# Ten unread products on TensorE between the first expert layer and the second attention

## The chip, the cores and the metric

The kernel runs on one core of one Trainium2 chip. The metric is the device time of one launch in microseconds (us). A core has five engines that work at the same time, each through its own queue in order: TensorE (PE, matrix products; its weight loads stand apart as PEld), VectorE (DVE), ScalarE (ACT), GpSimd (POOL) and SyncE (SP, which here only starts DMAs). [...]

## The reference

A network of two layers over 2708 tokens of width 256. Each layer is an attention over a graph given by the integer matrix adj (2708 x 2708, about 1.2% ones), and then a mixture of eight experts of which each token uses two. Both add to x, and both take x after a layer norm.

```python
# layer 0
x = x + elu(softmax(where(adj > 0, q k.T / 16, -9e15)) @ v)      # q, k, v of layernorm(x)
x = x + sum over a token's two best experts of w * (gelu(LN(x) W1 + b1) W2 + b2)   # hidden 1024
# layer 1
H = layernorm(x) @ W_fc + b_fc
s = (H @ w_att[:256])[:, None] + (H @ w_att[256:])[None, :] + b_att
x = x + softmax(where(adj > 0, s, -1e9), axis=1) @ H
x = x + sum over the two best experts, as above                    # hidden 512
```

In the second attention the first term of s is the same for a whole row, so it drops out of the softmax: the weight of a key is exp of its own score, masked by adj. The products of the change stand in none of these lines. What they compute is read by nobody.

## The kernel before, in words

**Tiling.** Tokens are cut into 22 tiles of up to 128 rows (NT), the last with 20. The first attention runs over blocks of 512 queries; the second over five groups of 6, 6, 4, 3 and 3 query tiles (GROUPS), each group going through all 22 key tiles, with one PSUM accumulator for each query tile. The expert layers run over slots: a slot is up to 128 tokens of one expert, whose rows are fetched from a table in DRAM (disp).

**Between the layers.** Each slot of the first expert layer ends with a scatter that adds its rows to xd0 in DRAM (L1197, on POOL's queue). `experts0.run` does 45 slots and, by a branch on a count, up to five more. `layer1_attention` then opens its pools over the memory of the layer that has ended: `kept` and `att1` on the right side of SBUF. `normed_rows` (L613) loads a tile of xd0 into kept (L615, SP), takes its statistics (L205 to L207, DVE), has POOL raise two numbers to the power -1/2 (L211), and writes the normalised tile xn (L217, DVE; four buffers, L617).

**The first group** does more than attend. For each key tile k, `columns` (L621) turns xn on TensorE (L223, two transposes against the identity `ident`), ACT copies the result out of PSUM into xT (L224), and DVE adds up its rows (L628). `values` (L631) multiplies xT by wfc (L635). ACT takes the exponent of one column (L641) and scales the rows by it (L642), and writes the part of the router (L643). POOL adds a bias to kept (L647) and makes the upper part of the rows (L650), DVE the rest (L652). `attend` (L677), three key tiles behind (LAG1), multiplies the masks by both parts (L685), which ACT has cast from one byte to float32r (L673). The loop is written so that the norm is two tiles ahead and the transpose one.

```python
            ahead = [normed_rows(t) for t in range(2)]
            cols = columns(0, ahead.pop(0))
```

The change stands just ahead of these two lines (L716, L717).

**What sets the order.** SP's instructions keep the order of the code (`manual_schedule` at L79). Inside `layer1_attention` the orders of TensorE, DVE, ACT and POOL are made by the framework's planner when the kernel is built: [...] nothing of the attention moves ahead of the end of the first expert layer. [...]

**PSUM.** The pool misc has two buffers of one bank (128 x 512 float32). Transposes, L635 and small products take turns in it. The accumulators of the second attention have six banks of their own.

**After the first group** the raw sums are divided and routed (`evict`, `finish`, `Experts.route`), tile by tile beside the next group's products, and scattered into the second layer's table (L950, POOL).

Of the kernel before, what the change touches and what calls it, by code (L numbers as in the profile page):

```python
# [9 lines left out]
F32 = mybir.dt.float32  # L10
# [10 lines left out]
P = 128  # L21
# [13 lines left out]
GROUP = 4  # L35
# [11 lines left out]
GROUPS = [6, 6, 4, 3, 3]  # L47

FIRST_MASKS = 2


FULL_AFTER = {14: 20, 16: 24}
# [13 lines left out]
def adj_ffn_kernel(ctx: ExitStack, tc: tile.TileContext, a: dict, out: bass.AP):  # L66
    nc = tc.nc
# [9 lines left out]
    misc = ctx.enter_context(tc.tile_pool(name="misc", bufs=2, space=PSUM))  # L77
# [4 lines left out]
    ident = const.tile([P, P], F32, name="ident")  # L82
# [117 lines left out]
    def norm_stats(src, r, deviation=None):  # L200

        st = small.tile([P, 6], F32, name="ln_st")
        mv = small.tile([P, 2], F32, name="ln_mv")
        rs = small.tile([P, 2, 2], F32, name="ln_rs")
        nc.vector.bn_stats(st[:r], src)  # L205
        nc.vector.bn_aggr(mv[:r], st[:r])
        nc.vector.scalar_tensor_tensor(  # L207
            rs[:r, 0], once_twice[:r, 0], mv[:r, 1:2], once_twice[:r, 1],
            op0=ALU.mult, op1=ALU.add,
        )  # L210
        nc.gpsimd.tensor_tensor(rs[:r, 1], rs[:r, 0], minus_half[:r], ALU.pow)  # L211
        if deviation is not None:
            nc.vector.tensor_mul(deviation, rs[:r, 0, 0:1], rs[:r, 1, 0:1])
        return mv[:r, 0:1], rs[:r, 1, 0:1], rs[:r, 1, 1:2]

    def normed(dst, src, mean, factor):
        nc.vector.tensor_scalar(dst, src, mean, factor, op0=ALU.subtract, op1=ALU.mult)  # L217
# [382 lines left out]
    def layer1_attention(mTs, kept, line, first_masks):  # L600
        with ExitStack() as scope:
            pool = scope.enter_context(tc.tile_pool(name="att1", bufs=2, side="right"))
# [10 lines left out]
            def normed_rows(t):  # L613
                r, x2 = ROWS[t], kept[:, t]
                nc.sync.dma_start(x2[:r], xd0[t * P : t * P + r, :])  # L615
                mean, factor, _ = norm_stats(x2[:r], r, spread_of[:r, t : t + 1])
                xn = rows.tile([P, D], F32, name="xn", bufs=4)  # L617
                normed(xn[:r], x2[:r], mean, factor)
                return xn

            def columns(t, xn):  # L621
                r = ROWS[t]
                xT = pool.tile([P, DC, P], F32, name="xT")
                if t < NT - 1:
                    to_columns(xT[:, :, :r], xn[:r], r)
                else:
                    tail_columns(xT, xn)
                nc.vector.tensor_reduce(sums_of[:, :, t], xT[:, :, :r], AX.X, ALU.add)  # L628
                return xT
# [65 lines left out]
            def finish(t, raw, total):  # L695
                r, x2 = ROWS[t], kept[:, t]
                rinv = over_sum(raw, r, VALUES, total)
                yield
                nc.vector.scalar_tensor_tensor(  # L699
                    x2[:r], raw[:r, :D], rinv, x2[:r], op0=ALU.mult, op1=ALU.add  # L700
                )
                nc.vector.scalar_tensor_tensor(
                    logits[:r, t], raw[:r, D:VALUES], rinv, logits[:r, t],
                    op0=ALU.mult, op1=ALU.add,
                )
                yield from experts1.route(t, x2, logits[:r, t])

            def evict(ts_, accs, total):
                for j, (t, acc) in enumerate(zip(ts_, accs)):
# [3 lines left out]
                    )  # L713
                    line.add(finish(t, raw, total))

            ahead = [normed_rows(t) for t in range(2)]  # L716
            cols = columns(0, ahead.pop(0))  # L717
            g0, total, since = 0, None, 0
            for g, wide in enumerate(GROUPS):
                if g == 2:  # L720

                    assert g0 >= FIRST_MASKS * GROUP
                    first_masks.close()


                    n = FULL_AFTER[experts1.early]
# [557 lines left out]
    with tc.tile_pool(name="mask", bufs=1) as mp, ExitStack() as first_masks:  # L1284
        mp_first = first_masks.enter_context(tc.tile_pool(name="mask_first", bufs=1))
        mTs = [
            (mp if b >= FIRST_MASKS else mp_first).tile([P, NT, nb], FP8, name=f"mT{b}")
            for b, (_, nb, _) in enumerate(BLOCKS)
        ]
        background.extend(  # L1290
            partial(nc.sync.dma_start, mTs[b], neighbours[b][:]) for b in range(len(BLOCKS))
        )
        experts0.run(line)
        early_rows.close()

        kept_pool = ctx.enter_context(tc.tile_pool(name="kept", bufs=1, side="right"))
        kept = kept_pool.tile([P, NT, D], F32, name="kept")
        layer1_attention(mTs, kept, line, first_masks)
        experts1.run(line)

    with tc.tile_pool(name="sum", bufs=1) as pool:
# [4 lines left out]
        def rows_of(dst, j, t, n, r):  # L1306
            t0 = j * N + t * P
            return dst[t0 : t0 + (n - 1) * P + r, :].rearrange("(t p) d -> p t d", p=r)

        for i, (t, n, r) in enumerate(parts_):  # L1310
            for j, queue in enumerate((nc.sync, nc.scalar)):
                start = queue.dma_start(ys[j][:r, t : t + n], rows_of(xd1, j, t, n, r))
# [44 lines left out]
```

## Time and profile before

| | us |
|---|---|
| median of three runs | 1307.23 |
| lowest, highest | 1306.99, 1308.36 |
| the profiled execution, its own time | 1317.0 |
| its span, first to last instruction | 1315.2 |
| first expert layer's last product begins (L1179, 26 in a row, 5.78 long) | 861.54 |
| second attention's first transpose (L223) | 879.86 |
| first attend (L685) | 891.69 |
| first group's last product (L232, the sum over all keys) | 949.68 |
| second expert layer's first slots (L1163) | 1081 |

Times within the trace count from the span's start. Rows of a timeline give start, length, engine, line, operation, what is written and read with shapes, the number of instructions merged, and in brackets the idle time before with what ended it. A float32 product appears as two MATMULs, and ends of MATMULs are modelled, so rows of one engine can overlap. A row for a stretch gives its length and, for PE, PEld, DVE, ACT and POOL, the busy time with the number of instructions, and then TensorE's granted clock (1.00 is full), the DMA share and GB/s.

### The profile page before, as it was taken

The numbers are of one execution on the slowest core, as the hardware profiler recorded it, in microseconds if no ns is written. First come the engines' busy times: TensorE is split into PE (matmuls) and PEld (weight loads), VectorE is DVE, ScalarE is ACT, GpSimd is POOL, SyncE is SP. The second block draws the span as 40 slices with busy tenths as digits, with TensorE's granted clock in tenths as the row PEclk, the third lists the DMA queues.
The fourth block names the chain that finished last, engine by engine and source line by source line (L and its number), as shares of the span: only waits on it lengthen the run. The fifth ranks groups of instructions, "written<-read, shape, count | busy, mean of one in ns | idle before, by whom it ended". The sixth has DMA issues, their size and how long they took to land. (4 is left out here: it accounts for less than half of the span.)

```text
span 1315.2 us, 20910 instructions
## 1 busy us (share of the span) xinstructions
PE 1200.9 (91%) x7074; PEld 963.3 (73%) x7074; DVE 533.9 (41%) x2087; ACT 447.4 (34%) x1296; POOL 419.4 (32%) x538
## 2 busy tenths in 40 slices
PE   7999999999999999999999999958987788999980
PEld 5776666656666675899999999947977667898870
DVE  7614733534625435632121212137554656312114
ACT  3222222112112222533333333326754557444430
POOL 4100110110210202343333333346343456555440
PEclk9999999999999999899999999978988999999995
DMA  8601365996937717265668645540004025545357
GB/s 275 210 1 65 105 176 145 245 235 171 262 91 181 149 57 289 83 197 142 213 213 273 202 128 147 168 104 1 1 28 175 33 73 177 170 139 163 100 169 257
DMA packets 107242, 197.83 MB, mean 150 GB/s; under 512 B 26753, under 2 KB 81718, under 8 KB 100986
## 3 DMA queue, kind: packets, MB, share of 16 engines
q1 hardware_dynamic: 77276, 110.09, 30.0%
q0 software_dynamic: 27040, 83.56, 20.0%
q10 hardware_dynamic: 2814, 2.77, 0.7%
q8 instruction: 59, 0.97, 0.3%
q14 instruction: 53, 0.43, 0.1%
HBM read 263.63 MB, written 66.12 MB: 251 GB/s over the span
## 5 line engine op out<-in xcount | busy, mean ns | idle before, releaser
L1163 PEld LDWEIGHTS mm<-xe,ring 128*128 128x128 f32 x2192 | 262.9, 193 | 30.5 <-ACT xe L1150 13.6
L1163 PE MATMUL mm<-xe,ring 128*128 128x128 f32 x2192 | 272.5, 278 | 13.7 <-ACT xe L1150 7.2
L1179 PE MATMUL acc<-ring,hT 128*128 128x256 f32 x1096 | 267.8, 382 | 4.6 <-ACT hT L1171 4.6
L1171 ACT ACTIVATE hT<-mm,ring 128x128 f32<-128x128 f32 x548 | 156.5, 369 | 255.8 <-issue 190.6
L1179 PEld LDWEIGHTS acc<-ring,hT 128*128 128x128 f32 x1096 | 195.8, 191 | 25.8 <-ACT hT L1171 5.3
L502 PE MATMUL acc<-v,p 128*128 128x257 f32 (+1 forms) x880 | 211.4, 392 | 0.0
L445 PE MATMUL s<-g,xnT 128*128 128x512 f32 x420 | 205.7, 604 | 4.4 <-DVE mT L457 4.3
L1185 DVE TENSOR_TENSOR y<-acc,bias 128x256 f32<-128x256 f32 x92 | 39.0, 424 | 364.5 <-PE acc L1179 361.0
L502 PEld LDWEIGHTS acc<-v,p 128*128 128x128 f32 (+1 forms) x880 | 155.0, 192 | 18.7 <-issue 0.8
L1092 POOL DMA_INDIRECT ring<-L_ffn_packed,weight_row x98 | 103.9, 1060 | 184.7 <-issue 141.4
L685 PE MATMUL acc<-parts,m 128*128 128x266 f32 x924 | 139.4, 308 | 21.9 <-ACT m L673 17.1
L685 PEld LDWEIGHTS acc<-parts,m 128*128 128x128 f32 x924 | 126.2, 198 | 30.2 <-ACT m L673 20.7
L950 POOL DMA_INDIRECT disp<-row,to x88 | 87.6, 996 | 148.2 <-DVE to L947 62.3
L211 POOL TENSOR_TENSOR ln_rs<-ln_rs,minus_half 128x2 f32<-128x2 f32 x88 | 65.6, 747 | 203.2 <-DVE ln_rs L207 183.2
L457 DVE TENSOR_SCALAR mT<-s 128x512 fp8e4<-128x512 f32 x105 | 72.1, 687 | 131.2 <-ACT p L456 130.1
L456 ACT ACTIVATE p<-s 128x512 f32<-128x512 f32 x105 | 62.3, 595 | 166.9 <-PE s L451 165.9
L445 PEld LDWEIGHTS s<-g,xnT 128*128 128x128 f32 x420 | 74.7, 190 | 50.8 <-issue 41.5
L1197 POOL DMA_INDIRECT xd<-y,xg x45 | 71.2, 1583 | 82.0 <-issue 38.2
L673 ACT CAST m<-mT 128x512 fp32r<-128x512 fp8e4 (+4 forms) x168 | 73.3, 471 | 35.0 <-PE acc L685 15.0
L451 PEld LDWEIGHTS <-apart 128*128 128x128 fp8e4 x420 | 32.9, 99 | 61.6 <-issue 61.6
L332 DVE TENSOR_SCALAR apart<-adj 128x677 fp8e4<-128x677 int32 x80 | 40.9, 515 | 52.5 <-DMA adj<-in_adj_dram 51.8
L1190 POOL DMA_INDIRECT xd<-y,xg x47 | 47.2, 1004 | 22.8 <-PE tp L1140 7.9
(223 smaller groups left out, 1132.3 us busy)
## 6 DMA issues: line engine op xcount, KB each, us to landing
adj<-in_adj_dram SPq DMA_DIRECT2D x84, 338.5 KB
L_ffn_packed<-in_L_ffn_W_dram SPq DMA_DIRECT2D x16, 1024.0 KB
xg<-disp SPq DMA_DIRECT2D x98, 129.0 KB
L_ffn_packed<-in_L_ffn_W_dram SPq DMA_DIRECT2D x16, 512.0 KB
neighbours<-mT SPq DMA_DIRECT2D x5, 1408.0 KB
mT<-neighbours SPq DMA_DIRECT2D x5, 1408.0 KB
xin<-in_x_dram SPq DMA_DIRECT2D x42, 128.0 KB
ring<-L_ffn_packed SPq DMA_DIRECT2D x4, 1154.0 KB
```

The lines of the kernel that those rows point to most:

```text
L211: nc.gpsimd.tensor_tensor(rs[:r, 1], rs[:r, 0], minus_half[:r], ALU.pow)
L445: nc.tensor.matmul(ps[:kr, :nb], xnT[:, c, k0 : k0 + kr], g[:, c, :nb], start=(c == 0), stop=False,)
L457: nc.vector.tensor_scalar(mT[:kr, k, :], ps[:kr, :nb], -BIG / 2, None, ALU.is_gt, saturate=False,)
L502: nc.tensor.matmul(accs[j][:r], p[keys, q0 : q0 + r], v[keys, k, :], start=(k == 0), stop=(k == NT - 1),)
L673: nc.scalar.copy(m[:, : q1 - q0], mTs[b][:, k, q0 - b * BN : q1 - b * BN])
L685: nc.tensor.matmul(acc[:r], masks[t], parts[:, k, i], start=(k == 0 and i == 0), stop=False,)
L950: nc.gpsimd.indirect_dma_start(disp[:], bass.IndirectOffsetOnAxis(ap=to[:r, j : j + 1], axis=0), rows2[j][:r], None,)
L1092: nc.gpsimd.indirect_dma_start(w, None, packed[:], bass.IndirectOffsetOnAxis(ap=self.weight_row[:, s : s + 1], axis=0), bounds_check=E * P ...
L1163: nc.tensor.matmul(ps[:, i, :], w[:, c * hidden + f * P : c * hidden + (f + 1) * P], xe[:, c, :], start=(c == 0), stop=(c == DC - 1),)
L1171: nc.scalar.activation(hT[:, f, :], ps[:, i, :], AF.Gelu, bias=w[:, b1 + f : b1 + f + 1])
L1179: nc.tensor.matmul(ps, hT[:, f, :], w[:, w2 + f * D : w2 + (f + 1) * D], start=(f == 0), stop=(f == hc - 1),)
L1197: start = nc.gpsimd.indirect_dma_start(xd[:], at, y, None, bounds_check=N - 1, oob_is_err=False, compute_op=ALU.add)
```

## The change

A constant PAUSE of 10, a tile `nothing` of 128 x 512 float32 in the pool att1, filled with ones by DVE, and ten products of it with the identity, all into one buffer of misc, `idle`. They stand after all function definitions of `layer1_attention` and ahead of its first load. Nothing reads `idle`, and nothing else of the kernel is changed.

```diff
+PAUSE = 10
...
+            idle = misc.tile([P, GROUP, P], F32, name="misc").rearrange("p g n -> p (g n)")
+            nothing = pool.tile([P, GROUP * P], F32, name="nothing", bufs=1)
+            nc.vector.memset(nothing, 1.0)
+            for _ in range(PAUSE):
+                nc.tensor.matmul(
+                    idle, ident, nothing, start=True, stop=True
+                )
             ahead = [normed_rows(t) for t in range(2)]
             cols = columns(0, ahead.pop(0))
```

## The prediction

> **What bounds the kernel now.** I read the page first, then the timeline of TensorE where the layers meet, then the same stretch for the other engines, then busy time and granted clock in equal stretches. The page says that TensorE is the bound nearly everywhere, and where it is not.
>
> ```profile
> PE 1200.9 (91%) x7074; PEld 963.3 (73%) x7074; DVE 533.9 (41%) x2087; ACT 447.4 (34%) x1296; POOL 419.4 (32%) x538
> PE   7999999999999999999999999958987788999980
> PEclk9999999999999999899999999978988999999995
> ```
>
> A slice is 32.9 us. The 5 in PE (slice 27, 855 to 888 us) has a 7 and an 8 in the clock row beside it: TensorE stands still there and is then slow. The timeline shows that the first expert layer ends and the second attention begins in this slice.
>
> ```profile
> 861.54 5.78 PE L1179 MATMUL acc<-ring,hT 128*128 128x256 f32 x26
> 879.86 0.66 PE L223 MATMUL misc<-ident,xn 128*128 128x128 f32 x2 [12.54 <-DVE ln_rs L207]
> 882.78 2.16 PE L635 MATMUL misc<-wfc,xT 128*128 128x273 f32 x4 [0.35 <-DMA kept<-xd]
> 891.69 2.15 PE L685 MATMUL acc<-parts,m 128*128 128x266 f32 x6 [3.25 <-POOL parts L650]
> 893.64 2.02 PE L635 MATMUL misc<-wfc,xT 128*128 128x273 f32 x4
> 896.60 1.19 PE L635 MATMUL misc<-wfc,xT 128*128 128x273 f32 x4
> ```
>
> TensorE is idle for 12.5 us, from 867.3 to 879.9. The same four instructions of L635 then take 2.16 and 2.02 us, but 1.19 us from 896.6 on: the clock. The timeline of the other engines says what the pause waits for.
>
> ```profile
> 870.76 1.56 POOL L1197 DMA_INDIRECT xd<-y,xg  x1 [3.19 <-issue]
> 875.06 10.64 SPq L615 DMA_DIRECT2D kept<-xd  x22
> 875.20 1.75 ACT L673 CAST m<-mT 128x512 fp32r<-128x512 fp8e4 x4 [12.31 <-DMA xd<-y,xg]
> 875.31 0.17 POOL L605 MEMSET parts<- 128x42 f32 x1 [2.99 <-DMA xd<-y,xg]
> 877.29 0.43 DVE L205 BATCH_NORM_STATS2 ln_st<-kept 128x6 f32<-128x256 f32 x1 [9.12 <-DMA kept<-xd]
> ```
>
> Most telling are the two middle rows after SP's. A cast of the masks and a memset read nothing of xd, yet both wait for the last scatter into xd and start at 875.2 and 875.3: they write tiles of pools opened over the memory of the expert layer. Whatever first writes a tile of that pool waits so. Finally the stretches, cut at the clock's own steps:
>
> ```profile
> 868.37:871.78 3.41, 0.00 (x0) 0.00 (x0) 0.00 (x0) 0.00 (x0) 1.02 (x1) 1.00 0.26 40
> 871.78:875.19 3.41, 0.00 (x0) 0.00 (x0) 0.00 (x0) 0.00 (x0) 0.54 (x1) 0.50 0.15 16
> 882.02:885.43 3.41, 3.00 (x8) 1.65 (x7) 2.29 (x9) 1.85 (x4) 2.56 (x4) 0.50 0.86 254
> 888.85:892.26 3.41, 0.57 (x1) 0.29 (x1) 1.90 (x8) 0.31 (x2) 2.40 (x5) 0.50 0.00 0
> 892.26:895.67 3.41, 3.32 (x11) 2.72 (x11) 2.72 (x13) 0.00 (x0) 2.80 (x5) 0.50 0.00 0
> 895.67:899.09 3.42, 3.42 (x22) 2.86 (x22) 2.29 (x7) 2.97 (x10) 1.99 (x5) 1.00 0.01 2
> ```
>
> The first column after the length is TensorE's busy time, the one after POOL's the clock. It falls to half at 871.8, after one empty stretch, and is back at 895.7, after the first full one; a stretch with 3.00 us busy did not bring it back.
>
> [...] here L262 filled 256 elements in 272 ns.
>
> **The change, part by part.** (1) The memset of nothing is a new first write in the attention's pool, on DVE, so it waits like the two rows above: start 875.3. At 272 ns per 256 elements, 512 take 0.54 us, so it ends at 875.8. It costs DVE nothing, since DVE has no work before 877.29; were that cover gone, 0.5 us.
>
> (2) The ten products. One float32 product is two MATMULs. Warm, L445 has the same form, four of its MATMULs (128x512) span 1.88 us, the last of them 0.592: (1.88-0.592)/3 = 0.43 us from start to start. At half clock twice that, 0.86 (L635 confirms the factor: 0.446 against 0.233). Twenty take 8.6 us warm, 17.2 us cold. They read nothing, so they begin at about 876.0, not at 867.3: cold. [...] Cold time c costs c/2 more than warm: 8.6+1.3 = 9.9 to 8.6+3.0 = 11.6 us, middle 10.7. The products end at 885.9 to 887.6; I take 886.7. The twenty weight loads of ident (190 ns warm) lie beneath the MATMULs.
>
> (3) What is queued behind them: the first transpose (L223), 879.9 before, now 886.7, and all of TensorE's queue. Who waits for it: ACT's copy of xT, DVE's sums over it (L628), and xn of the fifth tile, since xn has four buffers. The first four xn don't wait; they come at DVE's and POOL's alternating pace of 2 us a tile (before: 879.3, 881.3, 883.3, 885.5). The fifth came at 887.4, and the delayed transpose frees its buffer at 887.1. So the products cost the normalisation almost nothing if DVE's order lets it run ahead.
>
> (4) The start after that. From transpose to TensorE's next steady stretch: xT copied 0.9 us later, L635 0.95 to 2.04, ACT's table load (1.28 in the trace) meanwhile, its exponent and copy (0.17, 0.48) to 3.3, POOL's parts (0.41) at 3.8. From about 3.65 us after the transpose, at 890.4, TensorE should have work without a pause, warm. It has by then done three transposes (0.21 each) and one L635 pair (4 x 0.23 = 0.91): 1.5 us of warm work. So it is where one that began at 888.9 without a pause would be.
>
> The same for before: when L635 starts at 896.60, TensorE has done five transposes (1.05), three pairs (2.7) and twelve L685 (1.75): 5.5 us of warm work, so it stands as if begun at 891.1. From 904 to 940 it is busy without a gap, so it stays the bound. 891.1 - 888.9 = 2.2 us gained. With the products' bounds (-0.8, +0.9) and the start-up worked out by hand (0.8 in either direction): 0.5 to 3.5.
>
> (5) The rest. POOL's and SP's queues are passed by nothing; the new 2 KB per partition and the turn in misc cost nothing, TensorE itself being the earlier writer. Ten writes of one buffer by one engine in order should need no wait between them; with a wait of 51 ns, which is what an event instruction takes on PE's queue, and the 0.16 by which L445's last row is longer than its step, for each, 2.1 us would go, and with it the gain. After 949 the chain runs through DVE, POOL and scatters that all hang on the first group's results, so the gain passes to the end.
>
> The sum against the profiled execution: 1317.0 - 2.2 = 1314.8 (span 1315.2 - 2.2 = 1313.0). The runs' median of 1307.23 is 0.7% below that execution; 2.2 us remain 2.2. Forecast: 1305.0.
>
> **Rivals.** *The order is kept (slower).* [...] Before, L628's first sum stands at 882.14, ahead of the third xn (883.26). If that place is kept, DVE stands still until xT exists, 886.7+0.9 = 887.6; the third xn is 4.9 us late, and every alternation behind it, so POOL's parts come at 896.1, not 891.2, and L685 at 896.6. Then warm: L635's fourth pair at 899.9 instead of 896.60, 3.3 us slower: 1310.5, up to 1311.4 with the clock late by 0.9. It decides once the transpose falls behind the third xn while the sum is still ahead of it. Against it: DVE's rows stand by readiness (statistics of later tiles ahead of earlier xn), so a planner that counts the products moves the sum. *Products at once.* Were the memset not to wait, the products would run at 867.5 to 876.1, warm, and hide whole. But the transposes and pairs of 880 to 891 are some 2.7 us of warm work in 11: [...] the clock is lost again before 891.7. No gain, 1307.2. *Clock lost in the start-up.* [...] 1306.7. *A later stall.* The plan of the whole attention is made anew. At 973 a scatter of 4.37 us on the chain holds ACT's mask cast, and TensorE behind it; such a stall may vanish or double: 1305.0 - 4.4 = 1300.6, or 1309.4; with the best start (3.5 us), 1299.3.
>
> **How the numbers follow.** Forecast 0.42 (1303.7 to 1306.7, its own range); clock lost 0.05; order kept 0.17; at once 0.03; a stall less 0.23, one more 0.10. A measurement of this kernel tells about 0.2%, 2.6 us, from no change: below 1304.6 or above 1309.8. Faster: 0.17 of the forecast's 0.42 and the 0.23, so 0.40. Slower: 0.16 of the order's 0.17 and 0.05 of the stall's 0.10, so 0.21. Within: the rest, 0.39. The range goes from the best start with a stall less, 1299.3, to the kept order with a late clock, 1311.4.
>
> **What would show it.** A DVE memset at 875.3; 20 MATMULs from about 876.0, the first 0.86 apart, the last 0.43; L223 near 886.7 without a pause before it; four xn before the first L628; L635 at 0.91 a pair, clock 1.0 from 882 on; TensorE gapless from about 890.5; L232 (949.7 before) some 2 us earlier. Wrong would be: products at 867.5, a fall of the clock before 892, L685 at 896 or later, or a later L673 stall of another length.

## The result, and the profile after

The kernel with the ten products is slower: 1313.6 us (1312.14 to 1318.6) against 1305.87 us for the kernel before, each the median of six executions. The ratio is 1.0058, with a 95% interval of 1.0031 to 1.0085, so about 7.6 us of loss where 2.2 us of gain were forecast. On which chip these twelve executions ran is not known; after_xt4 below, which differs from this kernel by two buffers, was slower than before by 0.44% on one chip. The profiled execution took 1312.8 us (span 1311.0), less than the one profiled of before (1317.0). Single executions scatter by about 1%, so two profiles can't be set against each other by their spans. They can by a stage between two landmarks.

The page after looks much like the page before, the slice with the pause included:

```profile
PE 1205.4 (92%) x7094; PEld 965.0 (74%) x7094; DVE 535.6 (41%) x2088; ACT 446.3 (34%) x1296; POOL 420.6 (32%) x538
PE   7999999999999999999999999968986787999980
PEclk9999999999999999899999999988998989999995
```

Twenty MATMULs more, 4.5 us more busy time, a 6 where a 5 was. What happened is in the timelines. All lines of the attention have moved down by two (L217 is L219, L615 is L617, L650 is L652, L685 is L687). TensorE:

```profile
869.16 11.61 PE L724 MATMUL misc<-nothing,ident 128*128 128x512 f32 x20 [8.67 <-DVE nothing L722]
880.60 0.66 PE L225 MATMUL misc<-ident,xn 128*128 128x128 f32 x4
881.44 1.19 PE L637 MATMUL misc<-wfc,xT 128*128 128x273 f32 x4 [0.18 <-ACT xT L226]
886.21 2.19 PE L637 MATMUL misc<-wfc,xT 128*128 128x273 f32 x4 [3.35 <-ACT xT L226]
890.80 0.59 PE L687 MATMUL acc<-parts,m 128*128 128x266 f32 x1 [1.98 <-POOL parts L652]
893.09 2.02 PE L637 MATMUL misc<-wfc,xT 128*128 128x273 f32 x4
896.04 1.19 PE L637 MATMUL misc<-wfc,xT 128*128 128x273 f32 x4
...
949.12 1.16 PE L234 MATMUL misc<-wfc,spread 128*128 128x264 f32 x4
```

This execution reached the seam 6.9 us sooner, so times are compared from the first load of kept: 875.06 before, 868.17 here. From there the products begin at 1.0 us and the first transpose comes at 12.4 (before: 4.8). The first L637 pair runs at full clock, 1.19 us. Then TensorE stands still for 3.35 us, and the next two pairs take 2.19 and 2.02 us: the clock is lost a second time. The first L687 comes at 22.6 us (before: 16.6), the last product of the first group (L232, here L234) at 80.95 us (before: 74.62). The stretch from the first load of kept to that product is called **the stage** from here on. It lost 6.3 us. By the interval the whole lost 4.0 to 11.1 us, so the stage alone can account for it.

The rows of the other engines show how far the prediction held:

```profile
868.17 10.90 SPq L617 DMA_DIRECT2D kept<-xd  x22
868.30 1.75 ACT L675 CAST m<-mT 128x512 fp32r<-128x512 fp8e4 x4 [12.25 <-DMA xd<-y,xg]
868.62 0.48 DVE L722 MEMSET nothing<- 128x512 f32 x1 [7.28 <-POOL logits L610]
```

The memset waits as the cast beside it does, as forecast, and takes 0.48 us. And the stretches (length, then busy time with instructions of PE, PEld, DVE, ACT and POOL, then clock, DMA share and GB/s):

```profile
871.30:874.71 3.41, 3.41 (x5) 1.34 (x5) 2.05 (x11) 0.00 (x0) 2.11 (x3) 0.50 0.77 233
874.71:878.12 3.41, 3.41 (x9) 1.49 (x9) 1.80 (x9) 0.00 (x0) 2.49 (x4) 1.00 0.86 264
...
881.54:884.95 3.41, 1.31 (x6) 0.86 (x6) 2.37 (x11) 1.58 (x3) 1.39 (x3) 1.00 0.00 0
884.95:888.36 3.41, 2.15 (x5) 1.57 (x6) 2.32 (x11) 0.91 (x3) 3.08 (x5) 0.50 0.00 0
888.36:891.78 3.42, 1.05 (x4) 0.35 (x2) 2.88 (x10) 1.07 (x4) 2.05 (x4) 0.50 0.00 0
...
895.19:898.60 3.41, 3.41 (x22) 2.90 (x21) 2.79 (x8) 2.93 (x10) 2.35 (x4) 1.00 0.03 7
```

The products do bring the clock back, at 874.7, some 5.5 us after the first of them. The stretch with 1.31 us of TensorE's work, while it waits for the second pair, loses it again; it is back only at 895.2, when the first parts have come.

### The profile page after: what moved, and what is told of

It is laid out like the page before. It is cut to its first block, busy times and chain, and to the rows that moved or that the text cites. A ratio compares the mean times of both kernels' runs of the same rounds, so it can differ in the third digit from the quotient of the medians.

```text
span 1311.0 us, 20950 instructions
## 1 busy us (share of the span) xinstructions
PE 1205.4 (92%) x7094; PEld 965.0 (74%) x7094; DVE 535.6 (41%) x2088; ACT 446.3 (34%) x1296; POOL 420.6 (32%) x538
## 5 line engine op out<-in xcount | busy, mean ns | idle before, releaser
L1174 PEld LDWEIGHTS mm<-xe,ring 128*128 128x128 f32 x2192 | 267.0, 195 | 29.1 <-issue 16.8
L1174 PE MATMUL mm<-xe,ring 128*128 128x128 f32 x2192 | 276.0, 280 | 12.8 <-ACT xe L1161 5.2
L504 PEld LDWEIGHTS acc<-v,p 128*128 128x128 f32 (+1 forms) x880 | 152.9, 190 | 18.1 <-issue 0.8
L687 PE MATMUL acc<-parts,m 128*128 128x266 f32 x924 | 137.4, 305 | 20.6 <-ACT m L675 15.9
L687 PEld LDWEIGHTS acc<-parts,m 128*128 128x128 f32 x924 | 123.4, 194 | 29.8 <-ACT m L675 19.6
L213 POOL TENSOR_TENSOR ln_rs<-ln_rs,minus_half 128x2 f32<-128x2 f32 x88 | 65.4, 744 | 201.6 <-DVE ln_rs L209 178.2
```

The costliest lines, as they stand in the source:

```text
L504: nc.tensor.matmul(accs[j][:r], p[keys, q0 : q0 + r], v[keys, k, :], start=(k == 0), stop=(k == NT - 1),)
L687: nc.tensor.matmul(acc[:r], masks[t], parts[:, k, i], start=(k == 0 and i == 0), stop=False,)
L1174: nc.tensor.matmul(ps[:, i, :], w[:, c * hidden + f * P : c * hidden + (f + 1) * P], xe[:, c, :], start=(c == 0), stop=(c == DC - 1),)
```

## What the first rows of POOL show

What TensorE waits for at 890.80 is POOL's first **parts**: the upper bits of the first tile's rows, made by a CAST from the rows e that ACT has scaled. Here are ACT's scaling of these rows and POOL's timeline ahead of the CAST, in the kernel before, and then in the kernel after:

```profile
885.68 0.49 ACT L642 ACTIVATE e<-misc,e 128x264 f32<-128x264 f32 x1
...
888.60 0.70 POOL L211 TENSOR_TENSOR ln_rs<-ln_rs,minus_half 128x2 f32<-128x2 f32 x1
889.89 0.72 POOL L647 TENSOR_TENSOR kept<-kept,L_gnn_b_fc_b 128x256 f32<-128x256 f32 x1 [0.59 <-DVE xn L217]
890.57 0.70 POOL L211 TENSOR_TENSOR ln_rs<-ln_rs,minus_half 128x2 f32<-128x2 f32 x1
891.23 0.41 POOL L650 CAST parts<-e 128x265 fp32r<-128x265 f32 x1
```

```profile
886.05 0.49 ACT L644 ACTIVATE e<-misc,e 128x264 f32<-128x264 f32 x1
...
886.79 1.53 POOL L213 TENSOR_TENSOR ln_rs<-ln_rs,minus_half 128x2 f32<-128x2 f32 x2 [0.16 <-DVE ln_rs L209]
888.28 0.72 POOL L649 TENSOR_TENSOR kept<-kept,L_gnn_b_fc_b 128x256 f32<-128x256 f32 x1
889.69 0.70 POOL L213 TENSOR_TENSOR ln_rs<-ln_rs,minus_half 128x2 f32<-128x2 f32 x1 [0.69 <-DVE ln_rs L209]
890.34 0.76 POOL L652 CAST parts<-e 128x265 fp32r<-128x265 f32 x2
```

In neither does the CAST wait for its data, which is there 5.1 us ahead of it before and 3.8 us after; it waits for its turn. In the order as built, before has seven powers (L211) and six bias additions (L647) ahead of it, after has eleven and seven. No instruction of the change is on POOL; only the order built for it is another. Each power waits for DVE's statistics (0.69 us in the last row of L213 above), each addition for DVE's xn (0.59 us in the row of L647), so this queue moves at the pace of two engines that wait for each other. The first parts come at 16.2 us in the kernel before and at 22.2 us in the kernel after.

So the theory after the result was about **order**. The ten products hold the first transpose back in the plan too. While it waits, the planner sees DVE and POOL with nothing to do but statistics of later tiles, and puts those ahead. On the chip they are not done when the transpose comes, and what the attention needs first stands behind them. The orders are read from the traces; why the planner chose them is inferred. The rivals: **occupation** (TensorE's time for the products is lost as such, in any order), and a **later stage** (the loss lies after the first group, where the plan differs too). Against the last speaks that from the end of the stage on the profiled execution of after is the shorter, 361.9 against 365.5 us.

## The experiments

Each is timed against the kernel before on the same chip (for after see above), and its stage is taken from its one profile. Times in us count from the first load of kept.

| kernel | powers, additions ahead of first parts | first transpose, us | first parts, us | stage, us | ratio to before (95%) |
|---|---|---|---|---|---|
| before | 7, 6 | 4.8 | 16.2 | 74.6 | 1 |
| after | 11, 7 | 12.4 | 22.2 | 81.0 | 1.0058 (1.0031 to 1.0085) |
| pause1 | 5, 5 | 4.8 | 13.8 | 73.4 | 0.9995 (0.9971 to 1.0018) |
| early10 | 5, 5 | 4.8 | 13.8 | 73.5 | 1.0006 (0.9984 to 1.0028) |
| before_lead4 | 4, 4 | 4.8 | 11.5 | 69.8 | 0.9955 (0.9938 to 0.9972) |
| after_lead4 | 4, 4 | 12.0 | 15.3 | 72.1 | 0.9975 (0.9957 to 0.9993) |
| after_xt4 | 11, 7 | 12.0 | 22.2 | 81.9 | 1.0044 (1.0026 to 1.0063) |
| pause4 | 8, 7 | 6.7 | 18.1 | 76.6 | 1.0011 (0.9994 to 1.0029) |
| pause20 | 11, 7 | 20.5 | 26.6 | 85.8 | 1.0052 (1.0022 to 1.0082) |
| lead4_bf10 | 4, 4 | 4.9 | 11.7 | 70.6 | 0.9965 (0.9948 to 0.9981) |
| before_lead5 | 5, 5 | 4.9 | 13.6 | 72.4 | 0.9995 (0.9973 to 1.0016) |
| before_lead3 | 3, 3 | 4.8 | 11.2 | 69.8 | 0.9972 (0.9947 to 0.9997) |
| early10_lead4 | 4, 4 | 5.1 | 12.0 | 69.2 | 0.9961 (0.9947 to 0.9975) |

Kernels with the same order ahead of the first parts differ by up to 1.4 us (69.2 to 70.6 for four and four, leaving out after_lead4 with its late transpose), so smaller differences between two stages say little. The change of the stage, as a share of before's time, lies inside the interval of the ratio for every kernel but pause20. So the stage is enough to explain the whole in all but that one.

Take the stage less the first parts: it is 58.3 to 59.8 us for eleven of the thirteen kernels, whatever TensorE did before. The two exceptions, after_lead4 (56.9) and early10_lead4 (57.1), are the two in which the clock is full when the first parts come and stays full. In eight of the others the row that runs then, or the first L685, is at half speed: a pair of L635 of up to 2.19 us (1.19 at full clock), one L685 of 0.59 (0.37), or in early10 six of 1.70 (0.99). In pause1, before_lead5 and lead4_bf10 a pair that begins within 2.5 us of the first parts is slow again (1.92, 2.02 and 1.43 us). So a full clock that lasts goes with 1.2 to 2.9 us less.

**pause1: one product.**

```diff
-PAUSE = 10
+PAUSE = 1
```

> One product in place of ten. The stage meant is from the first load of kept (L615 of the kernel before, L617 of the kernel after) to the sum over all keys (L232, L234): 74.6 us before, 81.0 after. Order theory (the ten products hold the first transpose back, the planner then lets the statistics run ahead, and POOL's first parts stand behind more statistics): one product ends long before the transpose is due; in the order built for this kernel POOL's first parts stand behind five powers and five bias additions, before behind seven and six, so the stage should be about 4 us shorter than before, some 70.6. Occupation theory (TensorE's time for the products is lost as such): 1.7 us of product lie in the pause, so 74.6, as before. Later-stage theory (the loss lies after the first group): stage 74.6 to 81, the end slower by some us.

The first parts came at 13.8 us and the stage took 73.4, shorter than before by 1.3, not by 4. The sign is the order theory's, the size isn't: parts came 2.4 us sooner, and half of that was lost again behind them. Why isn't shown, and 1.3 us is within what stages of one order differ by. The whole time can't be told from before. One product and its memset are enough to give another plan.

**early10: ten products without the wait.**

```diff
-            nothing = pool.tile([P, GROUP * P], F32, name="nothing", bufs=1)
-            nc.vector.memset(nothing, 1.0)
...
+    nothing = const.tile([P, GROUP * P], F32, name="nothing")
+    nc.vector.memset(nothing, 1.0)
```

> All ten products, but the ones lie in a constant tile filled at the kernel's start, so the products don't wait for the last scatter and begin when the expert layer's last product ends. Order theory: the products take 8.6 us at full clock and are over before the transpose is due; the order of POOL and DVE is that of the kernel with one product, so the stage is some 70.6 us. Occupation theory: hidden whole, so as before, 74.6; the clock is lost again in the start-up either way. If ten products cost as such wherever they stand: 81.

The timeline of TensorE in early10:

```profile
862.88 7.89 PE L724 MATMUL misc<-nothing,ident 128*128 128x512 f32 x18
870.91 1.10 PE L724 MATMUL misc<-nothing,ident 128*128 128x512 f32 x2
876.22 0.69 PE L227 MATMUL misc<-ident,xn 128*128 128x128 f32 x2 [4.21 <-DVE xn L221]
879.27 2.16 PE L639 MATMUL misc<-wfc,xT 128*128 128x273 f32 x4 [0.31 <-DMA kept<-xd]
```

The products follow the expert layer's last product at once and at full clock, 0.43 us from one MATMUL to the next, and end 4.2 us ahead of the transpose. The stage is that of pause1, 73.5 us and not the 70.6 expected: next to one product, ten hidden ones show no cost. They bring nothing either. The first pair takes 2.16 us, 1.19 being its length at full clock: the clock is gone again by then. What a product is computed from sets where it can stand: the same ten went with a stage 6.3 us longer than before when they had to wait for a memset in a tile of the new pool.

**before_lead4: another order, no product.**

```diff
-        nc.gpsimd.tensor_tensor(rs[:r, 1], rs[:r, 0], minus_half[:r], ALU.pow)
+        power = nc.gpsimd.tensor_tensor(rs[:r, 1], rs[:r, 0], minus_half[:r], ALU.pow)
+        if behind is not None:
+            tc.add_manual_dep(power.ins, behind.name, ..., reason="no further ahead")
...
-                mean, factor, _ = norm_stats(x2[:r], r, spread_of[:r, t : t + 1])
+                mean, factor, _ = norm_stats(x2[:r], r, spread_of[:r, t : t + 1], split.get(t - 4))
...
-                nc.gpsimd.tensor_copy(parts[:r, t, 0, : VALUES + 1], e[:r])
+                split[t] = nc.gpsimd.tensor_copy(parts[:r, t, 0, : VALUES + 1], e[:r]).ins
```

The new dependency adds no wait (the first power behind the first parts begins at 878.28, as they end); it tells the planner that POOL's power for tile t stands behind POOL's parts of tile t-4.

> The kernel before with one thing more: the planner may not put POOL's power of key tile t ahead of POOL's parts of tile t-4. No product. Order theory: the first parts then stand behind four powers and four additions and come at about 11.7 us after the first load of kept instead of 16.2; the stage is 3 to 4.5 us shorter than before, 70 to 71.6. Occupation theory and later-stage theory say nothing of it: 74.6 if the place of parts in POOL's order doesn't matter.

Its POOL:

```profile
877.25 0.72 POOL L657 TENSOR_TENSOR kept<-kept,L_gnn_b_fc_b 128x256 f32<-128x256 f32 x1 [0.60 <-DVE xn L225]
877.91 0.41 POOL L660 CAST parts<-e 128x265 fp32r<-128x265 f32 x1
```

The rows e of the first tile are ready 11.1 us after the first load in both kernels. The CAST comes at 16.2 us before and at 11.5 here, and with it the stage is 4.8 us shorter and the whole 0.45% faster than before. The place of the CAST in POOL's queue is worth that much, with no product anywhere. The ratio is the lowest measured and beats both kernels; from several others, such as that of early10_lead4, it can't be told.

**after_lead4: ten products in that order.** The same edit on the kernel after.

> The kernel after with the same bound on POOL's order as before_lead4, so that the order differs little from that one and the products remain. Order theory: the first parts come some 4 us after the delayed transpose, at 16.3 us, and the clock is kept: the stage is 73 to 76 us, 5 to 8 less than after. Occupation theory: the products still hold TensorE for 11.6 us, so the stage stays near 81. Later-stage theory: no prediction for the stage.

TensorE in after_lead4:

```profile
867.49 11.16 PE L734 MATMUL misc<-nothing,ident 128*128 128x512 f32 x20 [8.29 <-DVE nothing L732]
878.49 0.66 PE L233 MATMUL misc<-ident,xn 128*128 128x128 f32 x4
879.33 1.19 PE L647 MATMUL misc<-wfc,xT 128*128 128x273 f32 x4 [0.18 <-ACT xT L234]
881.36 1.19 PE L647 MATMUL misc<-wfc,xT 128*128 128x273 f32 x4 [0.62 <-ACT xT L234]
882.52 1.04 PE L697 MATMUL acc<-parts,m 128*128 128x266 f32 x6
883.48 1.19 PE L647 MATMUL misc<-wfc,xT 128*128 128x273 f32 x4
```

And its POOL, where the CAST now waits for its data and not for its turn:

```profile
877.36 0.72 POOL L659 TENSOR_TENSOR kept<-kept,L_gnn_b_fc_b 128x256 f32<-128x256 f32 x1 [0.60 <-DVE xn L227]
881.75 0.41 POOL L662 CAST parts<-e 128x265 fp32r<-128x265 f32 x1 [3.66 <-ACT e L654]
```

The transpose is as late as in after (12.0 us), yet the stage is 72.1 us, 8.8 less than after and 2.5 less than before. All pairs take 1.19 us, as at full clock. So occupation, with all ten products in TensorE's way, costs 72.1 - 69.8 = 2.3 us against before_lead4. The other 8.8 us of after are order and the clock: the first parts come 6.9 us later there, and what follows them takes 1.9 us more. Occupation alone is refuted as the cause.

**after_xt4: four buffers for xT.** In after, ACT's copy of the third xT waits 2.63 us for DVE's first sum, which stands behind twelve statistics and six xn in DVE's order (five and two before), and ACT's scaling of the first rows is queued behind that copy. That could have been a cause of its own.

```diff
-                xT = pool.tile([P, DC, P], F32, name="xT")
+                xT = pool.tile([P, DC, P], F32, name="xT", bufs=4)
```

> The kernel after with four buffers for xT in place of two, so that ACT's copy of the third turned tile waits for no sum of DVE; the order on POOL is that of after (eleven powers and seven additions ahead of the first parts). Two causes stand in after: ACT's wait of 2.6 us, behind which the scaling of the first rows is queued, and POOL's order. If POOL's order alone sets the first parts, they come at 22 us as in after and the stage stays at 80 to 81 us. If ACT's wait is what sets them, they come 2.6 us sooner and the stage is about 78.

The rows e of the first tile were ready at 15.2 us, 3.2 sooner than in after, and still the first parts came at 22.16 us, those of after at 22.17. Two L637 pairs ran sooner (12.9 and 14.9 us), and nothing came of it; the stage took 81.9. Its rows of POOL are those of after, and TensorE waits for them:

```profile
896.01 0.70 POOL L213 TENSOR_TENSOR ln_rs<-ln_rs,minus_half 128x2 f32<-128x2 f32 x1 [0.68 <-DVE ln_rs L209]
896.66 0.76 POOL L652 CAST parts<-e 128x265 fp32r<-128x265 f32 x2
897.12 0.59 PE L687 MATMUL acc<-parts,m 128*128 128x266 f32 x1 [6.32 <-POOL parts L652]
```

POOL's order sets the first parts; ACT's wait was hidden beneath it.

**pause4 and pause20: the dose.** Only the constant differs.

> Four products. Cold they take 6.9 us from 1.0 us after the first load, so the first transpose moves from 4.8 to about 7.9 us. In the order built, eight powers and seven additions stand ahead of the first parts (one product: five and five; none: seven and six; ten: eleven and seven). Order theory: the first parts come between those of before (16.2) and after (22.2), at 17.5 to 20, and the stage is 76 to 79 us. Occupation theory: 3.1 us of delay, so 77.7 from before's 74.6, with no regard to parts.

Parts at 18.1 and a stage of 76.6, in the range of the order theory. The clock came back sooner than expected: from the first of the eight MATMULs (871.90) to the transpose (877.62) it is 5.7 us, against 6.9 at half clock throughout, and the transpose came at 6.7 us, not 7.9. With 1.9 us of delay the stage grew by 2.0, so this run alone doesn't tell the two theories apart; the place of parts fits both.

> Twenty products; the order on POOL is that of after (eleven and seven), so this doubles the time that TensorE is held and leaves the order. The ten more run at full clock and take 8.6 us, so the first transpose comes at 21.0 us. Occupation theory: 8.6 us more than after, a stage of 89.6. Order theory: in after the statistics were still running for 4.7 us after the transpose; that much of the delay is taken up, so the stage grows by 4 to 5.5 us, to 85 to 86.5.

Parts 26.6, stage 85.8, as the order theory had it: ten more products hold the transpose back by 8.0 us more and lengthen the stage by 4.9. In pause20 eight of the eleven powers are done when the transpose comes, and POOL stands still. Its next additions wait 5.75 us for xn and begin at 890.93, 0.9 us after the transpose (890.01) has begun: xn has four buffers, and four additions had been done. From the transpose to the first parts it takes 6.1 us, against 9.7 in after. The whole, at 1.0052, is 2.9 to 10.7 us over before, where the stage is 11.2 longer; a part of it may come back later. Where stays open: no profile of before is known to come from that chip.

**lead4_bf10: short products, to keep the clock.** before_lead4 with ten products of bfloat16 ones in front.

```diff
-            nothing = pool.tile([P, GROUP * P], F32, name="nothing", bufs=1)
+            nothing = pool.tile([P, GROUP * P], BF16, name="nothing", bufs=1)
...
-                    idle, ident, nothing, start=True, stop=True
+                    idle, ones, nothing, start=True, stop=True
```

> before_lead4 with ten bfloat16 products (ones by ones, 128x512), which take 0.43 us each at half clock, 4.3 in all, and so end about when the first transpose is due (4.8 to 5.6 us). The order on POOL is that of before_lead4. If a clock that is full at the start is worth something once the order is short, the first two L635 pairs take 1.2 us, not 2.2 and 2.1, and the stage falls from 69.8 to 68.3 to 69.5. If POOL and DVE alone set the start, it stays at 69.8; if the products get in the way, 70 to 71.

The stage was 70.6, no shorter than without products. That lies in the range given for products that get in the way, but the transpose came on time (4.9 us). The ten took 3.9 us up to it (873.20 to 877.08), 0.39 each, where 0.43 was the author's estimate. The first two pairs took 1.09 and 1.19 us, as meant. The first parts came at 11.7 as without products, and the third and fourth pair took 1.43 and 1.59 us, the six L697 between them 1.68 (0.99 after them): the clock was lost again. So a full clock ahead of the first parts, lost soon after them, gained nothing here.

**before_lead5, before_lead3: the place alone.** The edit of before_lead4 with 5 and with 3.

> The kernel before with the bound one tile looser: five powers and five additions ahead of the first parts, no product. The place of the first parts alone, without any product, is what is moved. Order theory: parts at 13.8 us, as with one product, and a stage of 73.4; without that theory 74.6 or 69.8.

> The bound one tile tighter: three powers and three additions. The rows of the first tile are ready at about 11 us, so the first parts can come no sooner than 11.2 against 11.5 with four: a stage of 69.3 to 70.5 if nothing else waits. If three tiles of lead are too few for POOL and DVE to keep TensorE busy, 71 or more.

With five, parts come at 13.6 and the stage takes 72.4 (73.4 expected); the whole can't be told from before. With three, parts gain 0.3 us more and the stage nothing: the CAST comes at 11.2 us, as soon as the rows e are ready, and there is nothing more to gain.

**early10_lead4: hidden products in the short order.**

> All ten products, hidden in the pause as in early10 (their ones lie in a constant tile), with the bound of before_lead4. Order theory: the order is that of before_lead4, and the products are over before the transpose, so the stage is 69.5 to 70.2 and the whole as fast as before_lead4 (0.4% under before). If ten products cost time as such, 71 or more.

Stage 69.2 us, 0.3 under what was expected, ratio 0.9961: as before_lead4. Ten products show no cost where they wait for nothing and hold nobody.

## Why the prediction was wrong

- **Part 1, the memset, was right.** It waits for the last scatter. Start 0.45 us after the first load of kept (0.24 forecast), length 0.48 (0.54).
- **Part 2, the products, was right.** 9.9 to 11.6 us were forecast for the twenty instructions; from the first of them (869.16) to the first transpose (880.60) it is 11.4. They are at half clock up to 874.71, for 5.5 us; how long that would last was the author's estimate. The transpose came 12.4 us after the first load of kept, 11.6 forecast.
- **Part 3 is where it failed.** "So the products cost the normalisation almost nothing if DVE's order lets it run ahead." DVE's order did let it run ahead, and that was the cost: POOL had eleven powers and seven additions to do before the first parts, which came at 22.2 us. The prediction's own times put them 3.4 us after the transpose, at 15.0. It asked which instruction waits for the transpose, and not what would be put ahead in its place on POOL. Part 5 says of POOL's queue only that it is "passed by nothing".
- **Part 4 inherits it.** It has POOL's parts start 3.4 us after the transpose and end at 3.8, as if POOL were free for them; they began 9.7 us after it. With POOL's order bound, after_lead4 has them at 15.3 - 12.0 = 3.3 us, as part 4 has it.
- **The gain of 2.2 us** is not borne out by that. The stage of after_lead4 is 2.5 us shorter than before's, but that this is near 2.2 is luck: the order alone, without a product, is worth 4.8 us (before_lead4), and in that order the ten products cost 2.3. Before was late at its start through POOL's queue, with the first rows lying ready for 5.1 us, and part 4 counts on that wait to be gone.
- **The rival "the order is kept"** had the sign and the wrong mechanism. It feared the first sum too early on DVE; it came too late, behind twelve statistics, and did not set the first parts (after_xt4). Its parts, at 896.1 or 21.0 us after the first load, lie near the 22.2 measured, but by another road. It would have cost 3.3 us; 6.3 were lost.
- **"Clock lost in the start-up"** did happen, from 16.8 to 27.0 us after the first load: first while the second pair waits for ACT and DVE, and then while TensorE waits for parts. In after_xt4, without that first wait, it was lost all the same: the second pair took 1.19 us, and behind the 6.32 us that TensorE waits for the parts the third took 2.02. Here a stretch of 3.41 us with 1.31 us of TensorE's work was followed by half clock. The traces give no level of work above which the clock stays: before, the stretch from 527.03 with 2.46 us of recorded work was followed by half clock, and after, the one from 1100.04 with 1.49 us was not. What this rival and the next say of the clock was the author's estimate.
- **"Products at once"** was run as early10. It gave no change that can be told, as forecast: 1.0006 (0.9984 to 1.0028).
- **A later stall** isn't needed for the sum: the stage's 6.3 us lie inside the interval of the whole. Part 5's fear of waits between the products is refuted too: in after, 3.41 us at full clock (874.71 to 878.12) hold nine of their MATMULs, 0.43 us apart as forecast without a wait, and the twenty more of pause20 hold the transpose back by 8.0 us, 0.40 each.
- **Two of its signs of being wrong came.** Set on before's times, the clock fell again at 891.9 and the first L685 came at 897.7.

## What to carry to other kernels

Where a planner makes the queues, an instruction that is put in is also an input to the plan: ask what the planner will do with the engines that the new work leaves idle, and read in the order as built what stands ahead of the instruction that the next stage starts from. Compare kernels by a stage between two landmarks when whole executions scatter by more than the effect. Look also for work that lies ready and waits for its turn: here the place in the queue was worth 4.8 us of the stage (before_lead4), and a full clock that lasts went with 1.2 to 2.9. Filler that is to hold a clock should not wait for memory of the stage that has ended, nor hold up the work behind it. No filler paid here: in the short order it cost 2.3 us where the stage had to wait for it, and changed nothing that can be told where it was hidden or short.

## What was not expected of the hardware

The same kernel before took 1306.6 to 1321.0 us in 67 runs on one chip (median 1313.1), 1300.2 to 1313.3 in 58 runs on another (median 1305.4) and 1309.0 to 1325.4 in 43 runs on a third (median 1316.9). Three runs had shown 1307.0 to 1308.4. An effect of 0.2% needs many runs on one chip, side by side.
